# TensorE multiplies ones in its waits during the setup of a filter and mixture-of-experts kernel

## The chip, the cores and the metric

The kernel runs on one core of a Trainium2 chip. The metric is the device time of one execution in microseconds, as the median of several runs. A separate execution was taken by the profiler; its span, from the first to the last instruction, is what the views of the profile show.

## The reference

Input x has 16 x 1024 tokens of 512 values. Cut to what matters:

```python
xn = layernorm(x)                                   # per token
# one number for the whole input, from its first 1024 values
sn = (s - s.min()) / (s.max() - s.min() + 1e-10)    # s: xn flattened
for sc in (2, 4, 8, 16, 32):
    blk = sn[:sc * sc]
    counts.append(max(sum(blk > blk.mean()), 1))
D = clip(-slope_of(log(counts), log(scales)), 1, 2)
# a filter of 512 frequencies that depends on D
filt = sin(omega*D + a*ka) * exp(1j * (omega*D - ka + b*ka**2))
x1 = ifft(fft(xn) * filt).real
lat = x1 @ W_el + b_el;  bits = lat > 0             # 24 bits a token
s = x1 + golay_correct(bits) @ W_le + b_le
g = silu(moe(xn))                                   # 8 experts, the best 2 of each token
out = x + s * g
```

Nothing of the filter is known until D is, and D needs five means and five counts over the first two tokens' values.

## The kernel before

All in one program with an order written by hand: each engine works through its instructions in the order in which the Python code issues them, and waits on semaphores for what another engine owes it. A first pass goes over the 128 tiles of 128 tokens (in 32 blocks of four, loaded with 1 MB each into five buffers): VectorE adds and subtracts halves of a tile (`total`, L443, and `fold`, L501 to L506), ScalarE sums squares for the variance (`spread`, L462), TensorE turns the tile (`transpose`, L513), ScalarE copies it (L515), TensorE multiplies it by the filter's matrices `cs`, `cd`, `cm` (`filt`, L529 to L532), ScalarE scales the result (L535), and SyncE's queue stores it in `yd`. Tokens are then sorted by their pair of experts and a second pass multiplies them with the experts' weights (L1254) and stores the result.

What the change touches is `setup` (L253), which runs once ahead of the first tile. The filter becomes a real matrix that is worked out on the chip:

1. VectorE forms five partial sums of the first values, held in `head` (L266 to L268). TensorE multiplies them by a matrix of ones, `st.all`, which adds over the partitions (L270), and by `st.own` (L273), into `pm`, a part of the first bank of the PSUM tile `py0`.
2. Meanwhile VectorE prepares the sine's arguments (`arguments`, L221 to L234). Then it compares with the means (`above`, L276), counts (L282), and TensorE adds the counts over the partitions (L283) into `pn` in the tile `py1`.
3. VectorE clears a buffer (L250, L251), takes the counts (L286), and clears 32 columns of the second bank of each of the two `py` tiles (L288). ScalarE takes logarithms (L289). VectorE makes D of them (L292, L293), then the arguments (L298 to L301), ScalarE the sine (L303), VectorE the gain of each frequency (L312) and with it the scaled basis (L315).
4. TensorE multiplies basis by scaled basis (L319: two products of 128 columns into `py0`; L324: four of 256 columns into `py1`). ScalarE copies the results to `cs`, `cd` (L336, L337) and `cm` (L342).
5. Between these steps the first tiles' `total`, `spread`, `fold` and `transpose` are placed; the small products of L347 to L351 complete the matrices.

`py0` and `py1` have two banks each, and the first pass uses them again for its products. The ones are set by GpSimd (L199) among the constants.

Of the kernel before, what the change touches and what calls it, by code (L numbers as in the profile page):

```python
# [17 lines left out]
P = 128  # L18
# [16 lines left out]
def kernel(  # L35
# [35 lines left out]
    nc = tc.nc  # L71
# [148 lines left out]
    def arguments():  # L220
        v, kf = nc.vector, st.kf  # L221
        kr = sp.tile([P, KC], F32, name="kr")
        v.tensor_scalar(kr, kf, -1.0, float(E), ALU.mult, ALU.add)
        ka = sp.tile([P, KC], F32, name="ka")
        v.tensor_tensor(ka, kf, kr, ALU.min)
        v.tensor_scalar(ka, ka, 1.0 / E, 1e-8, ALU.mult, ALU.add)

        st.by1 = sp.tile([P, 2, KC], F32, name="by1")
        st.by0 = sp.tile([P, 2, KC], F32, name="by0")
        v.tensor_scalar(st.by1[:, 0, :], ka, 0.5, 1.0, ALU.mult, ALU.add)  # L230
        v.tensor_mul(st.by1[:, 1, :], ka, ka)
        v.tensor_scalar(st.by1[:, 1, :], st.by1[:, 1, :], 0.1, 1.0, ALU.mult, ALU.add)
        v.tensor_scalar(st.by0[:, 0, :], ka, -math.pi, None, ALU.add)
        v.tensor_scalar(st.by0[:, 1, :], ka, -1.0, -0.5 * math.pi, ALU.mult, ALU.add)  # L234
# [14 lines left out]
    def clear(r):  # L249
        nc.vector.memset(r, 0.0)  # L250
        nc.vector.memset(bits_of(r)[:, :, L : L + 1], 1.0)  # L251

    def setup():  # L253
# [6 lines left out]

        cut = sp.tile([P, NS - 1, HW], F32, name="cut")
        sums = sp.tile([P, NS], F32, name="sums")
        every = head.unsqueeze(1)
# [1 line left out]
        v.tensor_reduce(sums[:, 0 : NS - 1], cut, AX.X, ALU.add)  # L267
        v.tensor_reduce(sums[:, NS - 1 :], head, AX.X, ALU.add)  # L268
        pm, pn = pys[0][:, 0, 0:NS], pys[1][:, 0, 0:NS]
        nc.tensor.matmul(  # L270
            pm[:, 0 : NS - 1], st.all, sums[:, 0 : NS - 1], start=True, stop=True
        )
        nc.tensor.matmul(pm[:, NS - 1 :], st.own, sums[:, NS - 1 :], start=True, stop=True)  # L273
        arguments()
        above = sp.tile([P, NS, HW], F32, name="above")
        v.tensor_tensor(  # L276
# [4 lines left out]
        cnt = sp.tile([P, NS], F32, name="cnt")  # L281
        v.tensor_reduce(cnt, above, AX.X, ALU.add)  # L282
        nc.tensor.matmul(pn, st.all, cnt, start=True, stop=True)  # L283
        clear(recs[0])
        ly = sp.tile([P, NS], F32, name="ly")
        v.tensor_scalar(ly, pn, 1.0, None, ALU.max)  # L286
# [35 lines left out]
        for i in range(2):  # L322
            for c in range(2):
                nc.tensor.matmul(  # L324
                    pys[1][:, i, 0:H], bas[:, 2 + c, i * P : (i + 1) * P], gbas[:, 2 + c, :],
                    start=(c == 0), stop=(c == 1),
# [22 lines left out]
        for i in range(2):  # L349
            for c in range(2):  # L350
                nc.tensor.matmul(  # L351
                    pw[:, 2 + i, :], cm[:, c, X + i * P : X + (i + 1) * P], wt[:, 2 + c, 0:L],
                    start=(c == 0), stop=(c == 1),
# [60 lines left out]
    pys = [ps_y.tile([P, 2, 512], F32, name=f"py{i}", bufs=1) for i in range(2)]  # L414
# [11 lines left out]
    def bits_of(rec):  # L426
        return rec.bitcast(BF16)[:, :, BITS : BITS + 32]
# [4 lines left out]
    st = Group()  # L432
# [635 lines left out]
    def pass_1():  # L1068
# [8 lines left out]
        constants()  # L1077
        more_constants()
        setup()
        rest = setup_code()  # L1080
        totals, spreads = list(range(6, NT)), list(range(6, NT))
# [484 lines left out]
```

## Time and profile before

| | |
|---|---|
| median of 3 runs | 1348.56 us (1347.62 to 1348.61) |
| the profiled execution | 1347.89 us |
| its span | 1346.1 us |
| TensorE busy | 1306.1 us (97%), 4752 matmul passes |
| VectorE, ScalarE, GpSimd busy | 909.7, 589.1, 769.1 us |
| mean granted TensorE clock | 0.991 |
| TensorE's first matmul | at 3.88 us |
| L319 starts, L324 ends | at 9.14 and 13.78 us |
| first filtered tile on TensorE (L529) | at 16.41 us |

An fp32 matmul of the program shows as two passes, each with a load of its weights (PEld). A timeline row gives start, duration, engine, line, operation, output and inputs, and in brackets the idle time before it and what ended it. PEclk is the clock that was granted to TensorE as a share of full speed; ahead of the first event that the profiler records, it prints 1.00.

### The profile page before, as it was taken

Reading aid. Unit: us, or ns where it says so; the run is one execution under the profiler, and the core shown is the slowest. Engines: PE = TensorE matmul, PEld = TensorE weight load, DVE = VectorE, ACT = ScalarE, POOL = GpSimd, SP = SyncE. Lnnn points to the kernel's source line nnn. Section 1 sums busy time; section 2 is a strip of 40 time slices with the busy share of each in tenths; the row PEclk is TensorE's granted clock in tenths of the full one; section 3 lists DMA queues with packets and bytes.
Section 4 is the critical chain, followed back from the end, with each engine's and each line's share of the span. In section 5 each row is a group of like instructions: output and inputs, shape, how many; then the busy total and the mean of one; then the engine's idle time right before and its main releaser. Section 6 shows DMA issues by size and latency. Waiting matters only on the chain.

```text
span 1346.1 us, 17641 instructions
## 1 busy us (share of the span) xinstructions
PE 1306.1 (97%) x4752; PEld 732.5 (54%) x4752; DVE 909.7 (68%) x2802; ACT 589.1 (44%) x1282; POOL 769.1 (57%) x743
## 2 busy tenths in 40 slices
PE   6998999998999999999999999999999999999996
PEld 5876888884444444444444444444444444444442
DVE  7887999984865888311111158777877887778775
ACT  7997999984222222222222223333333333333332
POOL 0042444547677553776543057777777777777731
PEclk9998999998999999999999999999999999999998
DMA  6998999846335332555445145555555565556531
GB/s 238 372 302 271 261 265 266 256 142 190 80 98 159 115 95 71 159 166 158 138 143 177 71 138 164 177 174 175 182 177 178 173 184 175 174 174 184 177 109 39
DMA packets 119289, 233.74 MB, mean 174 GB/s; under 512 B 37431, under 2 KB 71095, under 8 KB 115098
## 3 DMA queue, kind: packets, MB, share of 16 engines
q0 software_dynamic: 47264, 135.54, 34.0%
q1 hardware_dynamic: 71386, 96.88, 22.8%
q8 instruction: 42, 0.69, 0.2%
q14 instruction: 53, 0.43, 0.1%
q10 hardware_dynamic: 544, 0.21, 0.1%
HBM read 144.81 MB, written 87.75 MB: 173 GB/s over the span
## 4 chain that ended last, share of the span: by engine, by line
PE 84%; ACT 5%; issue 4%; DMA 3%; POOL 1%; DVE 1%; POOLq 0%; SPq 0%; ACTq 0%; DVEq 0%
PE pe L1254 63%; PE py L532 6%; PE pt L1222 3%; DMA yd<-yb 3%; PE pt L513 3%; PE py L529 2%; PE pg L1222 2%; ACT no L462 2%; PE py L530 2%; PE pg L1287 1%; ACT yb L535 1%; ACT pmt L515 1%; POOL out L1338 1%; PE pc L1275 1%; DMA xt<-in_x 0%
## 5 line engine op out<-in xcount | busy, mean ns | idle before, releaser
L1254 PE MATMUL pe<-w_sb,xt 128*128 x2104 | 938.6, 594 | 0.6 <-issue 0.6
L1254 PEld LDWEIGHTS pe<-w_sb,xt 128*128 128x128 f32 x2104 | 394.5, 190 | 416.2 <-issue 410.7
L1305 ACT ACTIVATE acc<-acc,yg 128x512 f32<-128x512 f32 x128 | 92.4, 722 | 419.4 <-DVE acc L1304 419.4
L787 POOL DMA_INDIRECT lists<-rec,dst x128 | 137.5, 1074 | 189.4 <-DVE sd L504 77.0
L1304 DVE SCALAR_TENSOR_TENSOR acc<-pe,yg,acc 128x512 f32<-128x512 f32 x101 | 75.7, 749 | 173.3 <-PE pe L1254 129.8
L1338 POOL DMA_INDIRECT out<-xg,toks x101 | 108.6, 1075 | 82.9 <-DVE xg L1333 56.7
L1211 DVE TENSOR_SCALAR xn<-xg,mean,entry 128x512 f32<-128x512 f32 x61 | 34.7, 569 | 166.7 <-PE pg L1222 166.3
L532 PE MATMUL py<-cm,pmt 128*128 128x288 f32 x512 | 146.9, 410 | 0.0
L1154 POOL DMA_INDIRECT yg<-yd,toks x101 | 109.1, 1081 | 52.0 <-issue 30.9
L1154 POOL DMA_INDIRECT xg<-in_x,toks x101 | 107.2, 1061 | 46.2 <-issue 27.5
L1301 ACT ACTIVATE acc<-pe,yg 128x512 f32<-128x512 f32 x101 | 68.9, 682 | 117.4 <-PE pe L1254 90.1
L535 ACT ACTIVATE yb<-py,rec 128x640 f32<-128x640 f32 x128 | 102.2, 798 | 24.1 <-PE py L532 14.3
L1154 POOL DMA_INDIRECT xg<-in_x,entry x88 | 88.6, 1006 | 30.9 <-issue 25.7
L1224 ACT COPY xt<-pg 128x512 f32<-128x512 f32 x56 | 32.8, 586 | 156.7 <-PE pg L1222 156.7
L1154 POOL DMA_INDIRECT part<-ed,adr_r x54 | 62.8, 1163 | 64.9 <-DMA ed<-res 48.8
L532 PEld LDWEIGHTS py<-cm,pmt 128*128 128x128 f32 x512 | 91.4, 192 | 13.8
L462 ACT ACTIVATE no<-xt,sum 128x512 bf16<-128x512 f32 x128 | 91.8, 717 | 0.9 <-DVE pp L443 0.9
L1333 DVE TENSOR_TENSOR xg<-mix,xg 128x512 f32<-128x512 f32 x128 | 88.6, 692 | 4.5
L1154 POOL DMA_INDIRECT entry<-lists,adr_i x61 | 63.3, 1038 | 46.5 <-DVE mean L1210 24.8
L1332 DVE TENSOR_TENSOR mix<-mix,acc 128x512 f32<-128x512 f32 x128 | 87.6, 685 | 0.8 <-ACT acc L1305 0.8
L1222 PEld LDWEIGHTS pt<-ident,xn 128*128 128x128 f32 x424 | 53.2, 142 | 58.5 <-issue 51.1
L515 ACT COPY pmt<-pt 128x512 f32<-128x512 f32 x128 | 73.7, 576 | 1.8 <-PE pt L513 1.6
(274 smaller groups left out, 1758.5 us busy)
## 6 DMA issues: line engine op xcount, KB each, us to landing
xt<-in_x SPq DMA_DIRECT2D x32, 1024.0 KB, 8.4
yd<-yb SPq DMA_DIRECT2D x32, 576.0 KB, 3.5
yd<-yb SPq DMA_DIRECT2D x32, 512.0 KB
ed<-res SPq DMA_DIRECT2D x61, 256.0 KB, 2.0
w_sb<-in_expert_w SPq DMA_DIRECT2D x8, 1024.0 KB, 9.1
yd<-rec SPq DMA_DIRECT2D x36, 64.0 KB, 5.5
lists<-rec,dst POOLq DMA_INDIRECT x128
xg<-in_x,toks POOLq DMA_INDIRECT x101
```

Source lines behind the costliest of these rows:

```text
L462: nc.scalar.activation(no, xts[g // TPT][:, g % TPT, :], AF.Square, bias=k.sum[:, j : j + 1], scale=-float(E), accum_out=k.sq2[:, j : j + 1],)
L515: nc.scalar.copy(pmts[g], pt)
L532: nc.tensor.matmul(py[:, 1, 0 : X + H], pmt[:, 2 + c, :], cm[:, c, :], start=(c == 0), stop=(c == 1))
L535: nc.scalar.activation(y_room(g), py[:, :, 0:WY], AF.Copy, scale=k.rec[:, j, 11:12])
L787: dma = nc.gpsimd.indirect_dma_start(out=lists, out_offset=bass.IndirectOffsetOnAxis(ap=st.dst[:, j : j + 1], axis=0), in_=st.rec.bitcast( ...
L1154: nc.gpsimd.indirect_dma_start(out=dst, out_offset=None, in_=src, in_offset=bass.IndirectOffsetOnAxis(ap=idx, axis=0), bounds_check=limit - 1,
L1222: nc.tensor.transpose(pt[:, c * P : (c + 1) * P], k.xn[:, c * P : (c + 1) * P], ident)
L1254: nc.tensor.matmul(pe.unsqueeze(1), k.xt[:, c, :], w_sb[:, bass.ds(e, 1), c, :], start=(c == 0), stop=(c == KC - 1),)
L1305: nc.scalar.activation(k.acc, k.acc, AF.Silu, bias=k.rec[:, 9:10])
L1332: nc.vector.tensor_mul(k.mix, k.mix, k.acc)
L1333: nc.vector.tensor_add(k.x, k.mix, k.x)
L1338: dma = nc.gpsimd.indirect_dma_start(out=of, out_offset=bass.IndirectOffsetOnAxis(ap=k.tok, axis=0), in_=k.x, in_offset=None, bounds_check ...
```

## The change

A helper `keep_going(n)` issues n products of the ones with themselves into `idle`, the first 128 columns of the second bank of `py0`; nothing reads them. It is called at three places of `setup`: three products ahead of the sums' matmuls, one behind them, and six behind the counts' matmul. The whole diff:

```diff
+        idle = pys[0][:, 1, 0:P]
+
+        def keep_going(n):
+            for _ in range(n):
+                nc.tensor.matmul(idle, st.all, st.all, start=True, stop=True)
+
         cut = sp.tile([P, NS - 1, HW], F32, name="cut")
         sums = sp.tile([P, NS], F32, name="sums")
...
         pm, pn = pys[0][:, 0, 0:NS], pys[1][:, 0, 0:NS]
+        keep_going(3)
         nc.tensor.matmul(
             pm[:, 0 : NS - 1], st.all, sums[:, 0 : NS - 1], start=True, stop=True
         )
         nc.tensor.matmul(pm[:, NS - 1 :], st.own, sums[:, NS - 1 :], start=True, stop=True)
+        keep_going(1)
         arguments()
...
         nc.tensor.matmul(pn, st.all, cnt, start=True, stop=True)
+        keep_going(6)
         clear(recs[0])
         ly = sp.tile([P, NS], F32, name="ly")
         v.tensor_scalar(ly, pn, 1.0, None, ALU.max)
         for py in pys:
             v.memset(py[:, 1, X + H : WY], 0.0)
```

Line numbers of the kernel before grow by seven to ten in `setup` and by ten behind it. All lines named here and in the prediction are those of the kernel before.

## The prediction

> **What bounds the kernel now.** I read the page first, then the chain of waits of the first microseconds, then the timelines of single engines there, and last the granted clock in narrow stretches. The page's chain says where a microsecond counts at all:
>
> ```profile
> PE 84%; ACT 5%; issue 4%; DMA 3%; POOL 1%; DVE 1%; POOLq 0%; SPq 0%; ACTq 0%; DVEq 0%
> ```
>
> Nearly all of it is TensorE work of the long stages behind the setup, which the change leaves alone. The change edits the first 10 us, which run once, so it can win or lose only what the setup's end moves. The chain there, in order of time (start us, us, what):
>
> ```profile
> 1.67 6.56 DMA xt<-in_x
> 8.29 0.31 issue
> ...
> 8.80 0.30 DVE w_sb L315
> 9.10 0.04 issue
> 9.14 1.23 PE py L319 x4
> 10.36 3.41 PE py L324 x8
> 13.78 0.87 PE pt L513 x4
> 14.64 0.02 issue
> 14.67 0.58 ACT pmt L515
> 15.25 0.72 ACT no L462 x2
> ```
>
> The reader is to see that the setup ends with the two products of the filter's matrix (L319, L324), 9.14 to 13.78, and that they follow the gain on VectorE (L315). Up to 8.25 the chain hangs on the first block of x, but VectorE's own work stands close behind that: it waited only 0.23 us for the block. The timeline of VectorE (start, us, engine, line):
>
> ```profile
> 4.90 0.20 DVE L276 TENSOR_TENSOR above<-head,py 128x40 f32<-128x40 f32 x1
> ...
> 6.24 0.17 DVE L286 TENSOR_SCALAR ly<-py 128x5 f32<-128x5 f32 x1
> 6.41 0.16 DVE L288 MEMSET py<- 128x32 f32 x2
> 6.68 0.17 DVE L292 SCALAR_TENSOR_TENSOR ly<-ly,slope 128x5 f32<-128x5 f32 x1
> ...
> 8.26 0.42 DVE L443 SCALAR_TENSOR_TENSOR pp<-xt 128x256 f32<-128x256 f32 x1 [0.23 <-DMA xt<-in_x]
> ```
>
> Then TensorE's speed. The profile prints a granted clock of 1.00 for these microseconds, yet L324 is slow: 8 passes over 256 columns start 0.427 us apart, while L532 takes 0.97 us for 4 passes over 288 columns (0.24 each). So the setup's products run at half clock; the pitch halves only at about 14.6. What the clock does in a gap can be read at 21.9 to 24.3, where TensorE stood idle (columns: stretch, then busy us of PE, PEld, DVE, ACT, POOL, then PEclk):
>
> ```profile
> 21.50:22.00 0.50, 0.41 (x4) 0.17 (x2) 0.50 (x4) 0.50 (x2) 0.00 (x0) 1.00 0.00 0
> 23.50:24.00 0.50, 0.00 (x0) 0.00 (x0) 0.50 (x5) 0.50 (x3) 0.00 (x0) 1.00 0.88 344
> 24.50:25.00 0.50, 0.50 (x5) 0.50 (x5) 0.49 (x2) 0.50 (x2) 0.00 (x0) 0.86 1.01 426
> 25.00:25.50 0.50, 0.50 (x3) 0.36 (x3) 0.18 (x2) 0.47 (x3) 0.00 (x0) 0.50 0.91 377
> 28.00:28.50 0.50, 0.50 (x4) 0.50 (x4) 0.50 (x3) 0.50 (x2) 0.00 (x0) 0.72 0.05 16
> ```
>
> An idle time of 2.37 us (21.91 to 24.28) was answered with half clock from 24.86 (0.86 and 0.50 in the rows), and full clock came back at 28.28, after 3.4 us of unbroken work.
>
> **The change, part by part.** It adds ten products of ones with ones, 128x128 fp32, two passes each: 20 passes. It removes and moves nothing else; the order of the built program shows the same instructions otherwise on every engine. From L319's rows such a pass is 0.213 us after the last at half clock and its result is there 0.42 us after its start; at full clock the pitch is 0.11 (0.24 x 128/288), the result 0.27 after (L513's rows at 16).
>
> *The first three* wait only for the ones that GpSimd sets by 1.30. Six passes end by 1.35 + 5 x 0.213 + 0.42 = 2.84; the sums come at 3.85. Nothing, covered by TensorE's first idle time; were the ones 1 us later, still nothing.
>
> *The one behind the sums.* The order of the changed program shows that the comparison `above` (L276) now waits for TensorE's sixth result, that of this product, not for the fifth: the five matmuls' signals are gathered into its own. L273's last pass starts at 4.51, so the new passes start at 4.72 and 4.94 and end at 5.36; `above` starts at 5.40 instead of 4.90. Everything behind it on VectorE, with the counts' matmul (5.60 to 6.10), moves by +0.50. At full clock it would be about +0.1; little work precedes it, so I take half clock.
>
> *The six behind the counts.* They write columns 0 to 127 of the second bank of py0, and the memset of L288 clears columns in the same bank. Before, that memset waits for nothing; in the changed program it waits for TensorE's 13th signal, the last of the six. Queued behind it on VectorE are the slope's product (L292), the dimension, the sine's arguments, the gain and L315, and who waits for those are ScalarE's sine and L319 itself. At half clock: the counts' passes at 6.10 and 6.34, twelve more from 6.55, the last starts at 8.90 and is done at 9.32; the memset starts at 9.36 instead of 6.41, +2.95. Should the clock come up at 7.0, ten of the twelve cost 0.11, and the memset starts at about 8.45, +2.04. The price of the six is in this wait; I take 9.1, near the slow end, since the work in front is broken by idle time from 2.8 to 3.85 and from 5.4 to 6.1.
>
> From the memset to L319 it was 9.14 - 6.41 = 2.73; the 0.23 of waiting for x falls away, as x has long come: 2.50. So L319 starts at 10.95 to 11.86 (taken: 11.6), not at 9.14. In these 2.5 us TensorE is idle again.
>
> *What it is worth to L319 and L324.* At half clock the two take 13.78 - 9.14 = 4.64. At full clock: 4 x 0.11 + 8 x 0.24 x 256/288 + 0.2 for the last result = 2.35, a gain of 2.3 at most, zero at least. [...] The row above says otherwise: 2.37 idle was enough. By it the clock is down before or in the block, and comes back after 3.4 us of work: it ends at up to 11.6 + 4.64 = 16.2. I go with the row, but [...] some of the block runs fast: 3.9 us, so the end is 15.5, against 13.78.
>
> *ScalarE.* It was free for its copy of L324's result (L342) at 12.81 and waited 1.00 us for it. Its sine and table load move with the memset: 12.81 - 6.41 = 6.40, less 0.4 of short waits that fall away, puts it there 6.0 us after the memset, at 14.45 to 15.4. So even with a fast block ScalarE is 14.45 - 13.81 = 0.64 later: a faster TensorE is not enough for a gain. Taken: copy at 15.55, +1.75; the transposes behind it (0.87 at half clock, 0.45 at full) leave +1.5 to +2.0 at L515, the end of the chain shown above. From there ScalarE, VectorE and TensorE carry the chain tile by tile with no wait for a load of x to 30 us (the chain names none), so I carry the delay to the end in full.
>
> The sum: 1347.89 us for the profiled execution (span 1346.1 and 1.8 around it) + 1.9 = 1349.8; the median of the runs, 1348.56, lies 0.67 above it, so 1350.5. This is +0.14%.
>
> **The rivals.** About 0.2%, 2.7 us, is what a measurement of this kernel can tell from no change.
>
> 1. *The wait costs its full price* (slower by over 0.2%): no help from the clock. Six products at half clock, memset at 9.36, L319 at 11.86, block 4.64, end at 16.50, and transposes at half clock: +2.7 at L515, 1351.3; if a further stretch at half clock falls on the tiles behind (as that of 24.86 to 28.28, worth 1.7) it is +4.4, 1353. It decides from the point at which the clock isn't back until the block's last quarter. For it: every row of the setup is slow, and the new gap is longer than the one that cost the clock. Against: the six products are 2.8 us of unbroken work just before.
>
> 2. *The clock is up when it matters* (the change does what it says): memset at 8.45, block at full clock, ScalarE the limit: +0.6, or 1349.2. Against it: the gap of 2.5 us.
>
> 3. *The delay is taken up later.* From 82 to 108 the chain hangs on stores of yd (11.18 and 14.81 us in its pieces), where compute waits for transfers; if these don't move with the setup, the result is 1348.6. Against it: from 26 to 28 the transfers stand still for want of free buffers, so they start later when compute does.
>
> 4. *Faster by over 0.2%*: halved clock from 24.86 (worth 1.7) doesn't occur and that from 106.8 to 113.6 is half as long (1.7), against case 2's loss of 0.6: -2.8, 1345.8. Nothing in the change aims there.
>
> **How the numbers follow.** My case (+1 to +2.7) 0.46, rival 1 0.34, rivals 2 and 3 together 0.16 (both within 0.2%), rival 4 0.04. So faster 0.04, same 0.62, slower 0.34. The likeliest case gives 1350.5, its own range is 1349.6 to 1351.3. The range for 8 in 10 reaches into rivals 2 and 3 below and to +4.2 above: 1348.2 to 1352.8.
>
> **What would show it.** In the changed profile: the memset of L288 (ten lines further down) with an idle time of 2 to 3 us before it on VectorE, released by TensorE; `above` 0.5 us later; six products from about 6.5 to 9; L319 at 11 to 12; the ones' passes 0.213 or 0.11 apart tell the clock, as do L324's (0.427 or 0.21). The step is wrong if the memset doesn't wait, if L319 starts before 10.5, or if L515 is later by 1.5 to 2.7 and the end isn't.

## The result and the profile after

The changed kernel took 1352.08 us (median of 17 runs, 1350.14 to 1355.48), the kernel before beside it 1348.94 us (17 runs, 1345.77 to 1352.77). The ratio is 1.0023, with a 95% interval of 1.0015 to 1.0032: 2.0 to 4.3 us slower. The profiled execution took 1353.28 us at a span of 1351.5.

The chain of waits of the first 20 us after the change (start us, us, what; line numbers are those of the changed kernel, L285 is the comparison, L298 the memset, L329 and L334 are the matrix's products):

```profile
4.80 0.65 PE py L268 x2
5.48 0.21 DVE above L285
...
6.18 0.59 PE py L292 x2
6.78 2.78 PE py L268 x12
9.55 0.07 issue
9.62 0.09 DVE py L298
...
11.79 1.22 PE py L329 x4
13.01 3.37 PE py L334 x8
16.40 0.59 ACT cm L352
16.99 0.49 ACT pmt L525
```

Where the chain before hung on the load of x up to 8.25, it now runs through the products of ones (L268) themselves: 0.65 us ahead of the comparison and 2.78 us ahead of the memset. The timeline of VectorE says who is waited for:

```profile
5.48 0.20 DVE L285 TENSOR_TENSOR above<-head,py 128x40 f32<-128x40 f32 x1 [0.59 <-PE py L268]
...
9.62 0.09 DVE L298 MEMSET py<- 128x32 f32 x1 [2.65 <-PE py L268]
```

And TensorE's timeline shows that the matrix's products gained nothing:

```profile
6.63 2.91 PE L268 MATMUL py<-all 128*128 128x128 f32 x12
11.79 1.22 PE L329 MATMUL py<-w_sb 128*128 128x128 f32 x4 [2.25 <-DVE w_sb L325]
12.80 3.56 PE L334 MATMUL py<-w_sb 128*128 128x256 f32 x8
```

Twelve passes take 2.91 us, close to 11 x 0.213 + 0.42 = 2.77 at the pitch of half clock; L334's eight take 3.56, as at half clock before (3.62). In this execution the clock came up at 16.18, as the block ended: the two passes of L523 that start at 16.20 take 0.38 us, where the first two of L513 before took 0.64. The first filtered tile (L529 before, L539 now) starts at 18.63 instead of 16.41, 2.22 us later.

### The profile page after: what moved, and what is told of

Its sections match the earlier page's. It is cut to its first block, busy times and chain, and to the rows that moved or that the text cites. A ratio compares the mean times of both kernels' runs of the same rounds, so it can differ in the third digit from the quotient of the medians.

```text
span 1351.5 us, 17680 instructions
## 1 busy us (share of the span) xinstructions
PE 1310.4 (97%) x4772; PEld 735.8 (54%) x4772; DVE 909.7 (67%) x2802; ACT 589.5 (44%) x1282; POOL 766.6 (57%) x743
## 4 chain that ended last, share of the span: by engine, by line
PE 78%; issue 6%; ACT 5%; DVE 4%; DMA 4%; POOL 2%; POOLq 0%; SPq 0%; ACTq 0%; DVEq 0%
PE pe L1264 61%; PE py L542 4%; PE pt L1232 3%; DMA yd<-yb 3%; PE pg L1232 2%; PE pt L523 2%; ACT no L472 2%; PE pg L1297 1%; PE py L539 1%; ACT yb L545 1%; PE py L540 1%; ACT pmt L525 1%; POOL out L1348 1%; POOL lists L797 1%; DMA lists<-rec,dst 1%
```

## The experiments

The rows "before" and "changed" of the table are the pair above. The other runs fall into three groups, each on one chip: other bank, six only, thirty and fuller; then before again, changed second, memset ahead and one in the other bank; then the remaining four. The scatter differed: the kernel before had a median of 1358.6 us in the first group (1350.8 to 1365.5), 1356.7 in the second, 1348.8 in the third. Ratios are to the kernel before of the same group; what they leave open is read from the traces. There the comparison and the memset of one kernel start within 0.01 us of each other in every trace; what follows moves with the clock and with the load of x. All starts below are from the timelines, in us:

| kernel | comparison | memset of py0 | L319 | L324 ends | first filtered tile | ratio [95%] |
|---|---|---|---|---|---|---|
| before | 4.90 | 6.41 | 9.14 | 13.78 | 16.41 | |
| before, again | 4.91 | 6.41 | 9.20 | 13.01 | 15.28 | 1.0013 [0.9994, 1.0033] |
| changed | 5.48 | 9.62 | 11.79 | 16.36 | 18.63 | 1.0023 [1.0015, 1.0032] |
| changed, second | 5.48 | 9.62 | 11.79 | 15.91 | 18.18 | 1.0007 [0.9988, 1.0025] |
| changed, third | 5.47 | 9.62 | 11.78 | 15.46 | 18.10 | 1.0012 [0.9997, 1.0027] |
| other bank | 4.84 | 6.34 | 9.27 | 12.42 | 15.06 | 0.9975 [0.9959, 0.9991] |
| other bank, again | 4.84 | 6.35 | 9.39 | 11.95 | 15.19 | 0.9993 [0.9982, 1.0003] |
| six only | 4.90 | 9.05 | 11.21 | 13.66 | 17.19 | 1.0021 [1.0005, 1.0037] |
| four only | 5.48 | 6.98 | 9.39 | 14.03 | 16.36 | 0.9999 [0.9985, 1.0013] |
| thirty | 5.47 | 15.21 | 17.37 | 19.83 | 23.17 | 1.0056 [1.0033, 1.0079] |
| memset ahead | 5.48 | 6.13 | 9.45 | 12.84 | 15.23 | 0.9986 [0.9966, 1.0005] |
| fuller | 4.97 | 6.47 | 9.25 | 11.98 | 14.87 | 0.9962 [0.9946, 0.9978] |
| fuller, again | 4.97 | 6.47 | 9.63 | 12.18 | 15.42 | 0.9993 [0.9981, 1.0005] |
| one in the other bank | 4.90 | 6.41 | 9.68 | 13.62 | 15.88 | 1.0012 [0.9995, 1.0028] |

Where the memset doesn't wait, L319 starts between 9.14 and 9.68: VectorE waited up to 0.78 us for the load of x there ("one in the other bank").

My theory (A) is that the loss is the two waits on py0's tile, and that the delay is carried to the end. The main rival (B) is that the ten products cost by themselves, wherever they write.

**Other bank.**

```diff
-        idle = pys[0][:, 1, 0:P]
+        idle = ps_t.tile([P, KC, P], F32, name="pt")[:, 0, :]
```

> The same ten products, but written into a transpose's PSUM tile, so that neither the comparison nor the memset of py0 waits for them. Theory A (the waits on py0's tile are the loss): the memset starts at about 6.4 us again, L319 at 9.1 to 9.3, and the six products before it bring the clock up earlier in L324, so the first filtered tile starts 0 to 1.2 us before that of the kernel before, and the end is 0 to 1.2 us faster than before. Theory B (the ten products cost by themselves, through TensorE's time, the clock or the longer program, wherever they write): the end stays 2 to 4 us slower than before.

The instructions and their order are the change's; only the PSUM tile of the idle products differs. The comparison and the memset are back in place without a wait, and TensorE's timeline has L334 faster from within its block (the clock came up at 10.76, and the eight passes take 2.14 us):

```profile
4.84 0.20 DVE L285 TENSOR_TENSOR above<-head,py 128x40 f32<-128x40 f32 x1
...
6.34 0.16 DVE L298 MEMSET py<- 128x32 f32 x2
```

```profile
5.99 2.91 PE L268 MATMUL pt<-all 128*128 128x128 f32 x12
9.27 1.22 PE L329 MATMUL py<-w_sb 128*128 128x128 f32 x4 [0.36 <-DVE w_sb L325]
10.28 2.14 PE L334 MATMUL py<-w_sb 128*128 128x256 f32 x8
```

The same twelve passes, with nobody waiting. The kernel is faster than before by 2.5 in a thousand, where B has it 2 to 4 us slower, so B falls: the products don't cost, the waits do. The gain of 3.4 us (0.0025 x 1358.6) is more than the setup's, though, which is 0.2 to 1.35 us against the two traces of the kernel before.

**Six only.**

```diff
-        keep_going(3)
...
-        keep_going(1)
```

> Only the six products behind the counts' matmul, in py0's second bank as in the change. Theory A: the comparison starts at 4.9 as before, the memset waits until about 9.0 (2.6 us later than before), L319 starts at about 11.2, the first filtered tile 1.6 to 1.8 us later than before, and the end 1.5 to 2.5 us later. Theory B (all ten cost alike): six tenths of the change's 3.1, so 1.9: the trace tells them apart by the wait before the memset, the end does not.

The memset waits as expected, and the comparison doesn't:

```profile
4.90 0.20 DVE L283 TENSOR_TENSOR above<-head,py 128x40 f32<-128x40 f32 x1
...
9.05 0.09 DVE L296 MEMSET py<- 128x32 f32 x1 [2.65 <-PE py L268]
```

So the six make the wait of 2.65, and the product behind the sums the other 0.58. In this execution the clock came up at 9.54, before the block, which therefore took 2.45 us (11.21 to 13.66); even so the first filtered tile is 0.8 later than before's first trace (1.6 to 1.8 was expected) and 1.9 later than its second. This comes close to the prediction's rival 2, in which the clock is up when it matters, seen in one execution: slower all the same, as ScalarE comes later to its copy, without waiting for TensorE, and the clock is halved again from 16.37 to 19.79 (0.50 in the stretch from 16.40 to 19.70), under the first filtered tile, whose L540 takes 1.89 us where L532 before took 1.13. The copy:

```profile
14.79 0.57 ACT L350 COPY cm<-py 128x512 f32<-128x512 f32 x1
```

**Thirty.**

```diff
-        keep_going(6)
+        keep_going(30)
```

> Thirty products behind the counts' matmul instead of six: the wait made long enough to see how a delay of the setup is carried to the end. The clock should come up within them; then some 16 of the 60 passes cost 0.213 and the rest 0.108 us, the memset starts at about 15 (8.7 later than before) and the first filtered tile is 7 to 9 us later than before. Theory A with the delay carried in full: the end is 7 to 9 us later. Theory C (a delay grows behind the setup, as 2.2 became 3.1): 10 to 12 later. Theory D (stores and loads behind the setup take it up): under 5 later.

The memset waited for the products until 15.21:

```profile
15.21 0.09 DVE L298 MEMSET py<- 128x32 f32 x1 [8.23 <-PE py L268]
```

The first filtered tile is 6.8 us later than in the first trace of the kernel before, and ScalarE's scaling of the 25th tile (L535, 74.9 us there) still 6.7 us later: nothing is taken up in the first 75 us. The end is 4.5 to 10.7 us later by the ratio, about 7.6 (the medians differ by 5.35). That fits a full carry; theory D, under 5, lies at the edge of the interval. It can't tell C from A.

**Fuller**, with six, two and seven products in the other bank.

> As the run with the other PSUM tile, with six, two and seven products in the three places, so that TensorE is hardly idle from 1.4 us to L319. Theory A: full clock by 5 to 9 us, L324's passes 0.22 us apart throughout, TensorE's block over at 11.6 instead of 13.8, and ScalarE (free for the copy at 12.8) the limit: the first filtered tile 1 to 1.3 us before that of the kernel before, the end 0.5 to 1.5 us faster. Theory B: slower than before by more than the change, as five products more are issued.

L324's eight passes take 1.89 us and end at 11.98, and ScalarE copies at 12.65 without waiting for them: a TensorE that is done still earlier would gain nothing here. The setup is 0.4 to 1.5 us shorter, the end 5.2 us faster by the ratio in this group (0.0038 x 1358.6; the medians differ by 4.8), far outside what the setup explains.

The second group was to check that surplus, with the kernel before run once more beside itself.

> The kernel before, run once more as if it were an experiment: every theory expects a ratio of 1.000 within some 0.15%, and the profile of the kernel before on the same chip as the others of this call. If the ratio is not 1, the comparison leans by as much, and the gains of 3.4 and 5.1 us for the runs with the other PSUM tile, twice what their setups show, are to be read with that.

The ratio is 1.0013, with an interval that holds 1. Its trace shows something else: L324 ended at 13.01 and the first filtered tile came at 15.28, 1.13 earlier than in the first trace of the same program, because the clock came up at 12.04 and not at 14.62 (L324's eight passes took 2.79 us, not 3.62). So a trace of the kernel before is by itself no fixed mark; and the two spans, 1346.1 and 1354.1, differ by more than the change does.

> The changed kernel on the chip of this call. Theory A with the delay carried in full: the first filtered tile 2.2 us later than that of the kernel before on this chip (1.7 to 3.2 with where the clock's drop and return fall), the end 2 to 3 us later. Theory C (growing behind the setup): 3 to 5 later.

The waits are as in the first trace, with the clock up at 15.24 (L334's eight passes took 3.10 us). The first filtered tile is 2.90 later than that of the kernel before in this group; the end's delay could not be told from 0, nor from the 2 to 3 us expected (1.0007, so -1.6 to 3.4 us).

**Memset ahead.**

```diff
+        v.memset(pys[0][:, 1, X + H : WY], 0.0)
         keep_going(6)
...
-        for py in pys:
-            v.memset(py[:, 1, X + H : WY], 0.0)
+        v.memset(pys[1][:, 1, X + H : WY], 0.0)
```

> All ten products into py0's second bank as in the change, but the memset of py0 is placed ahead of the six products, so that VectorE doesn't wait for them; that of py1 stays. The comparison still waits for the fourth product (+0.5). Theory A: the memset runs at about 6.2, L319 starts at 9.5 to 9.7, with full clock within the block; the first filtered tile is 0 to 1 us before that of the kernel before, and the end equal to 1.5 us faster. Theory E (the gains of the runs with the other tile came from turning the order of the two transpose buffers): equal to the kernel before or slower.

Moving one memset of 0.09 us takes the wait away with the products left in py0:

```profile
6.13 0.09 DVE L293 MEMSET py<- 128x32 f32 x1
...
9.45 1.22 PE L329 MATMUL py<-w_sb 128*128 128x128 f32 x4
```

TensorE is now the later one at L319 (no idle time before it), yet the block is shorter, 3.39 us against 4.64 and 3.81 in the two traces of the kernel before. The end is 0.9986, equal to the kernel before within its interval, and its median is 2.5 us below that of the changed kernel of the same group (1355.55 and 1358.09); theory E isn't needed for it.

**One in the other bank** (of the change's three places, only the one behind the sums).

> Only the product behind the sums, written into a transpose's tile: no wait for anyone, no warm clock, but the two transpose buffers change places for the rest of the pass as in the runs with the other tile. Theory A: within 0.1% of the kernel before. Theory E (turned buffers gain): 2 us or more faster than before.

1.0012 [0.9995, 1.0028]: turning the transpose buffers gains nothing. E falls.

The third group repeated three kernels on a chip with less scatter (the kernel before took 1344.9 to 1354.3 us there, 1350.8 to 1365.5 in the first group).

> The run with six, two and seven products in a transpose's tile, once more. Theory A: its setup is 0.4 to 1.5 us shorter than that of the kernel before (the latter's own moves by 1.1 us with the instant at which the clock comes up), so the end is 0.4 to 1.5 us faster, and the 5.1 us of its first measurement were mostly scatter of the chip. Theory F (a full clock from early on saves more behind the setup): again 3 us or more faster.

> The run with the change's ten products in a transpose's tile, once more. Theory A: 0.2 to 1.4 us faster than before. Theory F: again 2 us or more faster.

Both 0.9993: about 1 us faster, with intervals that just hold 1. The surplus of the first group did not come back. F falls; what made that group's gains so large stays open, and I call it the chip's scatter without having shown it.

> The changed kernel for the third time, beside the two above. Theory A with full carry: 2 to 3 us slower than before (the two measurements up to now gave 3.1 and 0.9), and 2.5 to 4 us slower than the two runs with the other tile. Theory B (the products cost, the waits don't): no slower than those two.

1.6 us slower than before, with an interval that just holds 1, and 2.6 slower than the two others of its group (0.0019 x 1348.8). With the other bank's run this is the direct pair: the same products, with the waits and without, and medians of 1350.91 and 1348.09 (the means are 3.1 us apart, twice the standard error of that is 1.5). B falls again.

**Four only** (the six left out).

> Only the three and the one product, in py0 as in the change; the six are left out. Theory A: the comparison starts at 5.4 to 5.5 instead of 4.9, the memset at about 7.0 without a wait for TensorE, L319 0.35 to 0.6 us later than before, and the end 0.3 to 0.6 later, which this measurement can't tell from 0; the trace can. Theory B (all ten cost alike): 1.2 later.

The comparison waits, the memset doesn't:

```profile
5.48 0.20 DVE L285 TENSOR_TENSOR above<-head,py 128x40 f32<-128x40 f32 x1 [0.58 <-PE py L268]
...
6.98 0.16 DVE L297 MEMSET py<- 128x32 f32 x2
```

L319 is 0.25 later than before, less than expected, since the 0.23 us of waiting for x is swallowed by the delay; the end is 0.9999.

## Why the prediction was right

The mechanism was as predicted: the memset of L288 waits for the last product in its bank, the rest of the setup queues behind it, and the kernel is slower by about the setup's delay, 2.0 to 4.3 us; the forecast's 1.9 lies just below that. Point by point:

*The first three* cost nothing: done at 3.01, and the sums' matmul started at 3.79, no later than before (3.88).

*The one behind the sums*: forecast +0.50, measured +0.58. The reason given was incomplete. In the run with the other bank the product stands in the same place, and the comparison starts at 4.84, before that product ends at 5.43. So the wait needs the shared tile, as the memset's does, though the comparison reads the tile's first bank and the product writes the second. Whether the program waits for the tile as a whole, or for a signal gathered over the products into it, was not separated.

*The six*: forecast for the memset 8.45 to 9.36, taken 9.1; measured 9.62 in all three traces. The slow end was right, with no pass of the twelve at full clock, plus 0.08 from the step before, 0.14 in the passes (2.91 us from the first start to the last end, not 2.77) and 0.04 in the signal. Taking 9.1 was too hopeful by 0.5.

*From there to L319*: forecast 2.50, measured 2.17. The path on VectorE and ScalarE was shorter here, without the 0.23 wait and with the logarithm and the sine's table load done at 8.52, ahead of the memset. The two errors nearly cancel: 11.79 against 11.6.

*The block*: forecast 3.9 between 2.35 and 4.64; measured 4.57, 4.12 and 3.68 in three traces, 4.12 on average. That a part of it would be fast was my estimate, with no row behind it. In the three traces the clock was up from 16.18, up from 15.24, and up from 9.44 to 12.85: how much of the block was fast differed with these instants, which no row told beforehand.

*The row of the idle gap* (2.37 us idle, then half clock): one trace went by it, another didn't. In the third trace of the change the clock was up at 9.44, and the gap of 2.25 us ahead of L329 was followed by half clock from 12.85, in the middle of L334; in the run with the six only the same gap of 2.25 us, with the clock up since 9.54, was followed by full clock up to 16.37. The lengths are the same and the places differ: the whole of the one gap lies behind 9.44, but 0.6 us of the other ahead of 9.54. That the place made the difference was not shown. The granted clock of the first (columns as above: stretch, then busy time of PE, PEld, DVE, ACT, POOL, then PEclk, the DMA engines' busy share and GB/s):

```profile
9.50:12.80 3.30, 1.05 (x8) 0.97 (x8) 3.00 (x20) 2.02 (x3) 0.00 (x0) 1.00 0.94 356
12.90:16.20 3.30, 3.30 (x13) 2.66 (x11) 2.70 (x15) 2.71 (x10) 0.00 (x0) 0.50 1.04 254
```

and of the second:

```profile
9.60:11.20 1.60, 0.00 (x0) 0.00 (x0) 1.49 (x10) 1.00 (x2) 0.00 (x0) 1.00 0.96 327
11.20:13.60 2.40, 2.39 (x13) 1.90 (x13) 2.33 (x13) 1.96 (x5) 0.00 (x0) 1.00 0.96 399
13.70:16.30 2.60, 2.11 (x16) 1.75 (x17) 1.40 (x8) 2.60 (x9) 0.00 (x0) 1.00 1.09 282
```

The reader is to see the idle TensorE at the head of both, and what the last row of each was granted: 0.50 and 1.00.

*ScalarE and the carry*: the copy of L324's result came at 16.40, not 15.55, and L515 at 16.88, +2.2 instead of +1.5 to +2.0. From there the delay was carried: 2.2 us at the first tile, 2.8 at the 25th (1.7 to 1.8 at both in the two other traces of the change). Behind some 80 us, where compute waits for stores, part of it can go. The 28th and 29th tiles in the second group's traces, first of the kernel before, then of the change:

```profile
79.60 0.80 ACT L535 ACTIVATE yb<-py,rec 128x640 f32<-128x640 f32 x1
83.33 0.79 ACT L535 ACTIVATE yb<-py,rec 128x640 f32<-128x640 f32 x1 [1.50 <-DMA yd<-yb]
```

```profile
82.49 0.80 ACT L545 ACTIVATE yb<-py,rec 128x640 f32<-128x640 f32 x1
84.84 0.79 ACT L545 ACTIVATE yb<-py,rec 128x640 f32<-128x640 f32 x1
```

The lag of 2.89 us shrinks to 1.51, as the kernel before waits 1.50 us for a store of `yd` and the change does not. This is the prediction's rival 3 at work in one pair. Farther on two traces of one program also drift apart (the kernel before's two spans are 1346.1 and 1354.1 us), so no single pair can show the rest, nor does the profiled pair's 5.4 us in the spans. That the delay reaches the end about in full rests on the medians, and stays less sure than the setup's part.

So the mis-sized term is the setup's delay, 1.9 in the sum. Against the trace it was worked out from it is 2.2. Against the mean of both traces of the kernel before (15.85) the three of the change (18.30 on average) are 2.5 us later, because in the trace that I read the clock came up at 14.62, in the other at 12.04. The three measured ratios, weighted by their intervals, give about 1.0018, or 2.5 us, and an interval of 1.6 to 3.4 by the same weighting, which is an estimate. The first comparison's 3.1 us has 2.2 and 2.5 in its interval.

Between my case and rival 1, which priced the same mechanism at +2.7, the runs don't decide. By the rival's own sign, a clock that is back only in the block's last quarter, the first two traces of the change are the rival's (back at 16.18 and 15.24, with blocks that end at 16.36 and 15.91); the third, with the first part of its block fast, is mine. The first comparison's median of 1352.08 lies above my case's own range, 1349.6 to 1351.3, and inside the wide one. Which of the two an execution shows was luck as far as the forecast goes. Rivals 2 and 4 did not occur in the changed kernel's traces, and rival 3's end, no loss, lies outside the first comparison's interval.

## What to carry to other kernels

Work put into idle time cost this kernel time through those who were made to wait for its result: written to another tile, the ten products held up neither the comparison nor the memset (4.84 and 6.34 us), written to py0 they held them up by 0.59 and 2.65 us. Look in the built order for waits that the filler adds, also on neighbours in the same PSUM tile that share no column with it, as these two, and for what queues behind them. Give filler a PSUM tile that no other engine touches soon, or move the neighbour ahead of it. And before making an engine faster (L324's eight passes took 2.14 us with the other bank, 3.62 before), ask who is next late: here ScalarE's copy waited 1.00 us for L324 in one trace of the kernel before and 0.17 in the other, which bounds the gain there, so that the best versions (other bank, fuller) are a microsecond faster than the kernel before, at the edge of what 14 to 22 runs can tell.

## What the runs showed of the hardware that I had not expected

The clock changed at other instants in each profiled execution of a program. In the first trace of the kernel before it came up at 14.62, went to half at 24.86 and came up again at 28.28; in the second it first came up at 12.04. So the block of the same program took 4.64 or 3.81 us, and its first filtered tile came at 16.41 or 15.28. In the three traces of the change the clock came up at 16.18, 15.24 and 9.44.

Nor did TensorE's busy time just before tell what the clock did next. In the run with the six only it was busy for none of the 1.60 us from 9.60 to 11.20 and for 2.39 of the 2.40 from 11.20 to 13.60, and full clock went on; then for 2.11 of the 2.60 us from 13.70 to 16.30, and half clock followed. What decides was not shown.
